# Products of constants in three dense attentions: in the first sequence's preparation, beside the first maxima and beside the last masked steps

## The chip, the cores and the metric

The kernel runs on one core of a Trainium2 chip. A core has TensorE (PE) for matrix products, with a separate path for loading weights (PEld), VectorE (DVE), ScalarE (ACT), GpSimd (POOL) and SyncE (SP), which mostly issues DMAs. Products are written to PSUM, eight banks of 2 KB for each of the 128 partitions; everything else stands in SBUF. The metric is the device time of one execution in microseconds (us). The profile also tells the clock that TensorE was granted, as a share of its full speed.

## What is computed

Four sequences of 512 tokens with 128 features, fp32, go through four layers, each a "ffn" block with a factor one half, an "attn" block and the same "ffn" block again:

```python
x = x + 0.5 * _L1_ffn_ref(_layernorm(x, axis=-1), ...)
x = x + _L1_attn_ref(_layernorm(x, axis=-1), ...)
x = x + 0.5 * _L1_ffn_ref(_layernorm(x, axis=-1), ...)
...
x = x + _L3_attn_ref(_layernorm(x, axis=-1), ...)
```

Two kinds of block hold a dense attention with 16 heads of 8 features. `_L1_ffn_ref` (used twice) is a causal attention with rotary positions, a layer norm, a mixture of eight experts of which each token uses two, and another layer norm:

```python
q_in = _apply_rope(xh, sin, cos).reshape(B, S, E)
q = (q_in @ Wq.T + bq).reshape(B, S, H, D)      # k from q_in too, v from x
scores = jnp.einsum('bqhd,bkhd->bhqk', q, k) * scale
scores = jnp.where(causal[None, None], scores, -inf)
attn = jax.nn.softmax(scores, axis=-1)
ctx = jnp.einsum('bhqk,bkhd->bqhd', attn, v).reshape(B, S, E)
x1 = _layer_norm(x + ctx @ out_proj_w.T + out_proj_b, ln1_w, ln1_b)
```

`_L3_attn_ref` is an attention over all 512 keys, without a mask, with rotary positions on q and k. The other blocks (local and block attentions, linear attention, experts, pattern layers) aren't touched here.

## The kernel before

One function, `dense_attention` (L720 to L872), holds the attention. It is called three times: by `l1_ffn` (L874) for layer 1's first and second ffn (called l1f and l1g below, `masked=True`), and by `l3_attn` (`masked=False`, called l3a). The program is a list of instructions for each engine, in the order in which the Python code issues them, apart from instructions that a scheduler may move on DVE; the products, the transposes and ScalarE's operations marked `by_order` keep the order of the code. Engines wait for each other with semaphores.

The 16 heads are worked four at a time, as 16 units (sequence b, group j). `qT` and `km` hold queries and keys transposed, 32 partitions for each of four heads, so that one 32-row product gives a head's scores. A unit has four steps, one for each tile of 128 keys; a step has two halves of two heads each. The steps of all units make one sequence of 64, and a loop from n = -LEAD (LEAD is 5) to 68 issues, for each n and half:

- `scores(n)`: `pk_at` <- qx, km: scores with keys on the partitions, 512 queries or, when masked, only those from the key tile on (512, 384, 256, 128). One buffer of two banks, "k".
- `maxima(n + 5)`: `pq_at` <- km, qT: scores of one tile of 128 queries in the order 0, 3, 2, 1; DVE takes each row's maximum into `nm` (L757 with the mask in one custom operation, L752 as a plain reduction of two heads without). Two buffers of two banks, "q".
- `weights(n)`: ACT takes the exponential of `pk_at` into `PT` (L787); when masked, POOL cuts the diagonal tile (L790).
- `with_values(n - 1)`: `po_at` <- PT, vh, summed over the four steps in one bank, "o".
- what stands due at this n: `queries` (`pm_at`, transposes of the maxima, then `qx` L768, the queries less their maxima), `end` (`pt_at`, division by the sums), `output`, `project`, the preparation of the next sequence, and the pieces of the next block, whose due times a hand-written plan gives (`tick()`).

PSUM is thus full: `MIX = dict(k=1, q=2, o=1, m=1)`, with two banks for each k and q buffer; "m" serves all the small products.

The preparation of a sequence is a list of functions with due steps. For the second to fourth sequence they are spread over the steps of the sequence before. For the first one, all that are due before step -5 are issued at once ahead of the loop (L849 to L852). In l1f and l1g these are six: `norm` and `scale` (layer norm of x into y), `features` (transposes `pt_y`, copy `yT` L241), `rotate` (`pw` <- yT times a permutation; `qin` on DVE L901 and L905), `queries` (`pq` <- qin, `qT` on ACT L911) and `keys` (`pk` <- qin, `kT` on ACT L917, four masked copies `km`). In l1g the first three find that the layer before has already made y and yT of sequence 0 (`ready`), and issue nothing. In l3a the six are `begin_sequence` (norm, `pt_y`, `yT`), first and second half of the rotated keys (`p` <- yT, DVE L1499 and L1505, POOL L1506), `mark` (km), and the two halves of the queries. `values` (`pv`, `vh` L715) is due at -4 and is issued in the loop.

So in steps -5 to -1 only maxima run, and in steps 59 to 63 (`n_steps - LEAD` and on) no maxima are left, only scores, weights and values, with the experts of the third sequence (`pl`, `pt_g`, `pb`, `pe`, and DVE's weighted sums L997) between them in l1f and l1g. `pe` takes its buffers from "q". In l3a other work of the block's end stands there.

`mm_in_order` (L163) issues a product that keeps its place on TensorE. `onesm` is a 128x128 tile of 1/128, `cst` the packed tile of constants. An fp32 product appears in the trace as two matmul records for each 128x512 product.

Of the kernel before, what the change touches and what calls it, by code (L numbers as in the profile page):

```python
# [29 lines left out]
B, S, D, H, HD = 4, 512, 128, 16, 8  # L30
# [73 lines left out]
def tile_macaron(ctx, tc, x_in, const_in, vec_in, w0_in, ws_in, ws3_in, w2f_in, w3_in, out):  # L104
# [17 lines left out]
    def bank(tag, name):  # L122
        n = 2 if tag in "kqd" else 1
        return psum["pool"].tile([P, n * 512], F32, tag=tag, name=name, bufs=psum["bufs"][tag])
# [10 lines left out]
    cst = keep.tile([P, CONST.n], F32, name="cst")  # L135
# [8 lines left out]
    onesm = keep.tile([P, P], F32, name="onesm")  # L144
# [15 lines left out]
    def transpose(dst, src):  # L160
        return nc.tensor.transpose(dst, src, ident[: src.shape[0], : src.shape[0]])  # L161

    def mm_in_order(dst, lhsT, rhs, start=True, stop=True):  # L163
        tc.keep_in_program_order(nc.tensor.matmul(dst, lhsT=lhsT, rhs=rhs, start=start, stop=stop))  # L164

    def transpose_in_order(dst, src):
        tc.keep_in_program_order(transpose(dst, src))

    def bcast(ap, n):

        return ap[:, :, None].to_broadcast([ap.shape[0], ap.shape[1], n])
# [47 lines left out]
    def by_order(i):  # L219
        if ordered["act"]:  # L220
            tc.keep_in_program_order(i)
# [37 lines left out]
    def tick(busy=False):  # L259
        clock[0] += 1  # L260
        for c in list(chains):
            while c[2] and clock[0] >= c[1] + c[2][0][0] and not (busy and c[2][0][2]):
                busy |= c[2][0][2]
                run(c)
# [415 lines left out]
    LEAD = 5  # L680
# [39 lines left out]
    def dense_attention(sb, prepare, finish, wo, masked, tiles=None):  # L720
# [6 lines left out]
        n_steps = TB * len(units)  # L727
# [3 lines left out]
        def seq(b):  # L731
            if b not in seqs:
                seqs[b] = {"vh": vhs[b % 2], "ao": sb.tile([P, TB, D], F32, tag="ao", name="ao", bufs=2)}
            return seqs[b]

        def maxima(step, half):

            (b, j), qt = units[step // TB], order[step % TB]
            qT, km = seqs[b]["q"], seqs[b]["k"]
            nk = (qt + 1) * P if masked else S  # L740
            pq = bank("q", "pq_at")
            for i in range(2):
                g = half * 2 + i
                mm_in_order(
                    pq[:, i * 512 : i * 512 + nk],
                    qT[32 * g : 32 * g + 32, ts(qt, P)], km[32 * g : 32 * g + 32, j, :nk],
                )
            nm = nms[j % 2]
            if not masked:
                a = nm[:, qt, 0:1]  # L750
                to = bass.AP(a.tensor, a.offset + 64 * half + HD * (j ^ 1), [list(a.ap[0]), [32, 2]])
                nc.vector.tensor_reduce(to, pq.rearrange("p (i n) -> p i n", i=2), AX.X, ALU.max)  # L752
                return
            for i in range(2):
                at = 64 * half + 32 * i + HD * (j ^ 1)
                s = sb.tile([P, S], F32, tag="s", name="s")
                nc.vector.tensor_tensor_reduce(  # L757
                    s[:, :nk], pq[:, i * 512 : i * 512 + nk], causal[:, S - nk :], 1.0, -BIG, ALU.add, ALU.max,
                    nm[:, qt, at : at + 1],
                )  # L760

        def queries(u):
            b, j = units[u]
            pm = bank("m", "pm_at")
            for qt in range(TB):
                transpose_in_order(pm[:, ts(qt, P)], nms[j % 2][:, qt, :])
            qx = sb.tile([P, S], F32, tag="qx", name="qx", bufs=2)
            nc.vector.tensor_add(qx, pm, seqs[b]["q"])  # L768
            qxs[u] = qx

        def scores(step, half):

            u, kt = step // TB, step % TB
            b, j = units[u]
            q0 = kt * P if masked else 0
            pk = bank("k", "pk_at").rearrange("p (i n) -> p i n", i=2)
            for i in range(2):
                g = half * 2 + i
                mm_in_order(
                    pk[:, i, q0:], seqs[b]["k"][32 * g : 32 * g + 32, j, ts(kt, P)], qxs[u][32 * g : 32 * g + 32, q0:]  # L780
                )
            return pk

        def weights(step, half, pk):
            q0 = step % TB * P if masked else 0
            PT = sb.tile([P, 2, S], F32, tag="PT", name="PT", bufs=4)
            by_order(nc.scalar.activation(PT[:, :, q0:], pk[:, :, q0:], AF.Exp, scale=SC8))  # L787
            if masked:
                d = PT[:, :, q0 : q0 + P]
                nc.gpsimd.affine_select(  # L790
                    d, d, pattern=[[0, 2], [1, P]], base=0, channel_multiplier=-1, compare_op=ALU.is_ge, fill=0.0
                )
            PTs[step, half] = PT

        def with_values(step, half):
            u, kt = step // TB, step % TB
            b, j = units[u]
            q0 = kt * P if masked else 0
            if kt == 0 and half == 0:
                pos[u] = bank("o", "po_at")  # L800
            PT = PTs.pop((step, half))
            for i in range(2):
                g = half * 2 + i
                at = (4 * g + j) * VW
                mm_in_order(
                    pos[u][32 * g : 32 * g + 32, q0:], seqs[b]["vh"][:, kt, at : at + 32], PT[:, i, q0:],
                    kt == 0, kt == TB - 1,
                )

        def end(u):  # L810

            b, j = units[u]
            ao, oT = seqs[b]["ao"], oTs.pop(u)
            pt = bank("m", "pt_at")
            for qt in range(TB):
                transpose_in_order(pt[:, ts(qt, P)], oT[:, ts(qt, P)])
            o3 = pt.rearrange("p (n c) -> p n c", c=32)
            rec = sb.tile([P, 16], F32, tag="rec", name="rec", bufs=2)
            nc.vector.reciprocal(rec, o3[:, :, HD])
            nc.vector.tensor_mul(  # L820
                ao.rearrange("p t (g c) -> p (t g) c", c=32)[:, :, HD * j : HD * j + HD], o3[:, :, 0:HD], bcast(rec, HD)
            )

        def output(b):
            pt = bank("m", "pt_ao")
            for t in range(TB):
                transpose_in_order(pt[:, ts(t, P)], seqs[b]["ao"][:, t, :])
            aoT = sb.tile([P, S], F32, tag="oT", name="aoT")
            by_order(nc.scalar.copy(aoT, pt))
            seqs[b]["aoT"] = aoT  # L830

        def project(b):
            po = bank("m", "po_ao")
            for t in range(TB):
                mm_in_order(po[:, ts(t, D)], seqs[b]["aoT"][:, ts(t, P)], wo)
            finish(b, po.rearrange("p (t d) -> p t d", d=D))
            del seqs[b]

        oTs = {}
        for u, (b, j) in enumerate(units):  # L840
            n = TB * u
            later.setdefault((n - 1, 0), []).append(lambda u=u: queries(u))
            later.setdefault((n + 5, 1), []).append(lambda u=u: end(u))
            if j == 3:
                later.setdefault((n + 6, 1), []).append(lambda b=b: output(b))
                later.setdefault((n + 7, 1), []).append(lambda b=b: project(b))
            if j == 0:
                for at, f in prepare(b, seq(b)["vh"], seq(b)):
                    if b or at >= -LEAD:  # L849
                        later.setdefault((n + math.floor(at), int(at % 1 * 2)), []).append(f)  # L850
                    else:
                        f()  # L852

        for n in range(-LEAD, n_steps + 5):
            for half in range(2):
                pk = scores(n, half) if 0 <= n < n_steps else None
                if n + LEAD < n_steps:
                    maxima(n + LEAD, 1 - half)
                if pk is not None:
                    weights(n, half, pk)  # L860
                if 1 <= n <= n_steps:
                    with_values(n - 1, half)
                    if half and n % TB == 0:
                        u = n // TB - 1
                        oTs[u] = sb.tile([P, S], F32, tag="oT", name="oT")
                        by_order(nc.scalar.copy(oTs[u], pos.pop(u)))
                fs = later.pop((n, half), ())
                tick(bool(fs))
                for f in fs:
                    f()  # L870
# [1122 lines left out]
```

## Time and profile before

| what | us |
|---|---|
| median of 4 runs | 2941.87 |
| lowest, highest | 2938.86, 2943.68 |
| the profiled execution | 2939.49 |
| its span | 2937.8 |
| mean granted clock of TensorE | 0.862 |
| busy: PE, PEld | 2277.1 (78%), 1181.2 (40%) |
| busy: DVE, ACT, POOL | 1810.8 (62%), 1245.1 (42%), 911.2 (31%) |

The profile is of one execution; the span runs from its first to its last instruction, and all times of rows are counted from the span's start. In a row of the timeline stand the start, the duration of the group, engine, line, operation, the tile written and the tiles read, their sizes (a product is rows*columns of the weights, then partitions x elements of the result), how many records the group has, and in brackets how long the engine had been idle before it and what ended that. The line of most products is that of the helper (L164, transposes L161), so products are told apart by the tile that they write. A row of windows has the window, its length, the busy time and count of PE, PEld, DVE, ACT and POOL, the granted clock, the DMA share and GB/s.

Where the three attentions lie in the trace: l1f's preparation from 422 us (its first product, `pt_y`), its loop from 436 to 764; l1g's from 911 and 919 to 1261; l3a's from 2125 and 2140 to about 2500.

The chain of work that ended last is 51% PE, 23% DVE, 10% ACT, 8% POOL and 6% issue; its largest parts are `pk_at` (10% of the span), `po_at` (6%) and the exponentials (4%). The largest groups of instructions:

```profile
L787 ACT ACTIVATE PT<-pk_at 128x1024 f32<-128x1024 f32 (+3 forms) x384 | 310.8, 809 | 561.0 <-PE pq_at L164 475.2
L164 PE MATMUL pk_at<-qx,km 32*128 32x512 f32 (+3 forms) x1536 | 373.9, 564 | 61.4 <-ACT PT L787 56.4
L164 PE MATMUL po_at<-PT,vh 128*32 128x512 f32 (+3 forms) x1536 | 338.3, 523 | 3.5 <-POOL PT L790 3.3
L757 DVE CUSTOM_DVE_ANT_0 s<-pq_at,cst 128x384 f32<-128x384 f32 (+3 forms) x512 | 248.6, 486 | 100.0 <-PE pq_at L164 89.1
```

### The profile page before, as it was taken

Reading aid. Unit: us, or ns where it says so; the run is one execution under the profiler, and the core shown is the slowest. Engines: PE = TensorE matmul, PEld = TensorE weight load, DVE = VectorE, ACT = ScalarE, POOL = GpSimd, SP = SyncE. Lnnn points to the kernel's source line nnn. Section 1 sums busy time; section 2 is a strip of 40 time slices with the busy share of each in tenths; the row PEclk is TensorE's granted clock in tenths of the full one; section 3 lists DMA queues with packets and bytes.
Section 4 is the critical chain, followed back from the end, with each engine's and each line's share of the span. In section 5 each row is a group of like instructions: output and inputs, shape, how many; then the busy total and the mean of one; then the engine's idle time right before and its main releaser. Section 6 shows DMA issues by size and latency. Waiting matters only on the chain.

```text
span 2937.8 us, 46900 instructions
## 1 busy us (share of the span) xinstructions
PE 2277.1 (78%) x17558; PEld 1181.2 (40%) x17558; DVE 1810.8 (62%) x4776; ACT 1245.1 (42%) x2682; POOL 911.2 (31%) x1700
## 2 busy tenths in 40 slices
PE   4277538889678898958576678988689999689987
PEld 2145213333333333338456645555322222355553
DVE  4656476676566666554564477777455564677773
ACT  3054303433332433313232266766224444477773
POOL 1022012332122222212321387775100000677661
PEclk8588759999787999768776789999779999899998
DMA  3042010000000000007104510000000000100000
GB/s 133 0 152 81 0 58 1 1 1 1 1 1 1 1 1 4 4 8 266 60 9 168 165 30 22 21 21 14 1 1 1 1 1 1 24 23 20 22 21 11
DMA packets 33771, 99.12 MB, mean 34 GB/s; under 512 B 6184, under 2 KB 12072, under 8 KB 33032
## 3 DMA queue, kind: packets, MB, share of 16 engines
q1 hardware_dynamic: 30616, 88.03, 9.1%
q0 software_dynamic: 2496, 5.12, 0.8%
q8 instruction: 138, 2.26, 0.3%
q10 hardware_dynamic: 432, 2.98, 0.3%
q14 instruction: 89, 0.73, 0.1%
HBM read 66.88 MB, written 14.55 MB: 28 GB/s over the span
## 4 chain that ended last, share of the span: by engine, by line
PE 51%; DVE 23%; ACT 10%; POOL 8%; issue 6%; DMA 1%; POOLq 0%; DVEq 0%; ACTq 0%; SPq 0%
PE pk_at L164 10%; PE po_at L164 6%; ACT PT L787 4%; PE pa L164 3%; PE pag L164 3%; PE po L164 3%; PE pe L164 3%; PE p_qk L164 2%; DVE t L1599 2%; PE pq_at L164 2%; DVE t L1596 2%; PE pg L164 2%; PE pv L164 2%; POOL t L1603 2%; PE pt L161 2%
## 5 line engine op out<-in xcount | busy, mean ns | idle before, releaser
L787 ACT ACTIVATE PT<-pk_at 128x1024 f32<-128x1024 f32 (+3 forms) x384 | 310.8, 809 | 561.0 <-PE pq_at L164 475.2
L164 PE MATMUL pk_at<-qx,km 32*128 32x512 f32 (+3 forms) x1536 | 373.9, 564 | 61.4 <-ACT PT L787 56.4
L164 PE MATMUL po_at<-PT,vh 128*32 128x512 f32 (+3 forms) x1536 | 338.3, 523 | 3.5 <-POOL PT L790 3.3
L757 DVE CUSTOM_DVE_ANT_0 s<-pq_at,cst 128x384 f32<-128x384 f32 (+3 forms) x512 | 248.6, 486 | 100.0 <-PE pq_at L164 89.1
L1548 ACT ACTIVATE s<-s,nm,rn 128x128 f32<-128x128 f32 x512 | 245.5, 483 | 2.4 <-DVE nm L1654 2.2
L790 POOL TENSOR_SCALAR_AFFINE_SELECT PT<-PT 128x256 f32<-128x256 f32 x256 | 107.0, 419 | 431.6 <-ACT PT L787 431.5
L164 PE MATMUL pq_at<-km,qT 32*128 32x384 f32 (+3 forms) x1024 | 226.7, 532 | 12.7 <-DVE nm L757 6.2
L164 PEld LDWEIGHTS pk_at<-qx,km 32*128 32x128 f32 x1536 | 121.8, 193 | 270.3 <-ACT PT L787 205.5
L752 DVE TENSOR_REDUCE nm<-pq_at 128x2 f32<-128x1024 f32 x128 | 156.2, 1225 | 104.3 <-PE pq_at L164 103.8
L1603 POOL TENSOR_TENSOR t<-t,t 128x1024 f32<-128x1024 f32 x64 | 151.3, 2364 | 135.8 <-DVE t L1599 135.4
L161 PE MATMUL pt_y<-ident,y 128*128 128x128 f32 x224 | 55.1, 378 | 156.9 <-DVE y L214 85.4
L164 PE MATMUL pq_at<-km,t 32*128 32x512 f32 x512 | 149.4, 689 | 7.0 <-DVE nm L752 4.9
L164 PE MATMUL p_qk<-w,hT 128*128 128x512 f32 x256 | 141.8, 681 | 11.0 <-DVE t L1599 9.1
L164 PEld LDWEIGHTS po_at<-PT,vh 128*32 128x32 f32 x1536 | 56.2, 110 | 225.4 <-issue 149.1
L161 PE MATMUL pt<-ident,s 128*128 128x128 f32 x640 | 92.8, 292 | 67.4 <-POOL s L1666 35.5
L241 ACT COPY yT<-pt_y 128x512 f32<-128x512 f32 x56 | 32.7, 584 | 258.1 <-PE pt_y L161 211.3
L1666 POOL TENSOR_TENSOR s<-s,sm 128x1024 f32<-128x1024 f32 x64 | 121.4, 1896 | 47.5 <-DVE sm L1665 39.4
L1596 DVE TENSOR_TENSOR t<-p_qk,w 128x1024 f32<-128x1024 f32 x64 | 78.3, 1224 | 70.2 <-ACT sq L1548 69.8
L1548 ACT ACTIVATE sq<-p_qk 128x1024 f32<-128x1024 f32 x64 | 65.5, 1024 | 127.4 <-PE p_qk L164 70.6
L161 PEld LDWEIGHTS pt<-ident,s 128*128 128x128 f32 x640 | 78.3, 150 | 99.6 <-POOL s L1666 52.5
L161 PEld LDWEIGHTS pt_y<-ident,y 128*128 128x128 f32 x224 | 34.9, 173 | 188.5 <-issue 113.1
L1290 DVE SCALAR_TENSOR_TENSOR hT<-pa,w,sg 128x128 f32<-128x128 f32 x184 | 51.8, 345 | 84.8 <-ACT sg L1289 63.9
(424 smaller groups left out, 5196.0 us busy)
## 6 DMA issues: line engine op xcount, KB each, us to landing
w<-in_w2f_dram SPq DMA_DIRECT2D x46, 836.0 KB, 6.3
vb<-v SPq DMA_DIRECT2D x112, 128.0 KB, 2.2
skew<-qe SPq DMA_DIRECT2D x16, 512.0 KB, 3.0
rel<-skew SPq DMA_DIRECT2D x64, 128.0 KB, 3.3
w<-in_w_dram SPq DMA_DIRECT2D x1, 4147.0 KB, 12.3
w<-in_w_dram SPq DMA_DIRECT2D x1, 3200.0 KB
od<-o SPq DMA_DIRECT2D x46, 64.0 KB, 4.7
yd<-y SPq DMA_DIRECT2D x8, 256.0 KB, 2.3
```

Source lines behind the costliest of these rows:

```text
L161: return nc.tensor.transpose(dst, src, ident[: src.shape[0], : src.shape[0]])
L164: tc.keep_in_program_order(nc.tensor.matmul(dst, lhsT=lhsT, rhs=rhs, start=start, stop=stop))
L752: nc.vector.tensor_reduce(to, pq.rearrange("p (i n) -> p i n", i=2), AX.X, ALU.max)
L757: nc.vector.tensor_tensor_reduce(s[:, :nk], pq[:, i * 512 : i * 512 + nk], causal[:, S - nk :], 1.0, -BIG, ALU.add, ALU.max, nm[:, qt, at ...
L787: by_order(nc.scalar.activation(PT[:, :, q0:], pk[:, :, q0:], AF.Exp, scale=SC8))
L790: nc.gpsimd.affine_select(d, d, pattern=[[0, 2], [1, P]], base=0, channel_multiplier=-1, compare_op=ALU.is_ge, fill=0.0)
L1290: nc.vector.scalar_tensor_tensor(hT[s][:, c, :], pa[:, ts(c, P)], b1[:, c : c + 1], sg, ALU.add, ALU.mult)
L1548: tc.keep_in_program_order(nc.scalar.activation(*args, **kw))
L1596: nc.vector.tensor_mul(by_head(t1), by_head(p3), over(tab[:, 0]))
L1599: nc.vector.tensor_mul(by_head(t2[:, :, a]), by_head(p3[:, :, z]), over(tab[:, 1, :, a]))
L1603: nc.gpsimd.tensor_add(t1, t1, t2)
L1666: nc.gpsimd.tensor_mul(s, s, bcast(sm, P))
```

## The change

A helper issues a product of two constants into a fresh PSUM tile that nothing reads, `n` columns wide. `dense_attention` calls it in three places: with 512 columns (S) in bank "o" after each of the six functions of the first sequence's preparation, whether or not the function issued anything; with 256 columns in "o" in both halves of the five steps that have maxima alone; and, in the masked attentions only, with 256 columns in "q" in both halves of the last five steps. In the loop it comes after the maxima and ahead of the weights and of `with_values`. That is 6 + 10 + 10 products in each of l1f and l1g and 6 + 10 in l3a, 68 in all. What the kernel computes stays the same.

```diff
+    def idle_product(tag, n):
+
+        mm_in_order(bank(tag, "idle")[:, :n], onesm, cst[:, :n])
+
...
                         later.setdefault((n + math.floor(at), int(at % 1 * 2)), []).append(f)
                     else:
                         f()
+                        idle_product("o", S)
 
         for n in range(-LEAD, n_steps + 5):
             for half in range(2):
                 pk = scores(n, half) if 0 <= n < n_steps else None
                 if n + LEAD < n_steps:
                     maxima(n + LEAD, 1 - half)
+                if n < 0:
+                    idle_product("o", S // 2)
+                elif masked and n_steps - LEAD <= n < n_steps:
+                    idle_product("q", S // 2)
                 if pk is not None:
                     weights(n, half, pk)
```

## The prediction

> **What bounds the kernel now.** I read the page's forty slices first, then the stretches around the three attentions window by window, then TensorE's timeline inside them.
>
> ```profile
> PE   4277538889678898958576678988689999689987
> PEclk8588759999787999768776789999779999899998
> ```
>
> A slice is 73.4 us. Slices 5 and 28 (about 367 and 2057 us on) hold l1f's preparation and the work ahead of the last attention; the granted clock is 0.5 and 0.7 there, and the whole run's mean is 0.862. So the kernel is bound by chains of products at changing speed, and a stage's start and end are where it is slow. Windows over the tail of the first masked attention (start, length, busy time and instructions of each engine, clock):
>
> ```profile
> 731.37:734.78 3.41, 3.41 (x24) 1.48 (x24) 2.50 (x11) 0.88 (x3) 0.81 (x2) 1.00 0.00 0
> 734.78:738.20 3.42, 2.00 (x14) 0.59 (x12) 2.10 (x11) 1.84 (x2) 0.42 (x1) 1.00 0.00 0
> 738.20:741.61 3.41, 3.15 (x8) 0.69 (x8) 0.00 (x0) 1.49 (x3) 0.81 (x2) 0.50 0.02 5
> 741.61:755.26 13.65, 13.65 (x51) 5.14 (x49) 1.24 (x3) 2.96 (x5) 1.63 (x4) 0.50 0.00 0
> 755.26:758.68 3.42, 3.42 (x6) 1.14 (x4) 0.00 (x0) 0.00 (x0) 0.00 (x1) 0.50 0.00 0
> 758.68:762.10 3.42, 3.42 (x21) 1.28 (x20) 2.37 (x7) 0.38 (x1) 0.41 (x1) 1.00 0.01 2
> ```
>
> After one window with only 2.00 us of products the clock halves, and stays halved for six windows, four of which have PE busy to the last hundredth. TensorE is then the bound, and DVE waits for it:
>
> ```profile
> 755.23 3.68 PE L164 MATMUL pe<-ws,yT 128*128 128x512 f32 x4
> 758.95 2.28 DVE L997 SCALAR_TENSOR_TENSOR y<-pe,g,y 128x128 f32<-128x128 f32 x6 [6.18 <-PE pe L164]
> ```
>
> The other two cold places are the preparations, l1f's and then l1g's on TensorE's timeline, and l3a's end on ScalarE's:
>
> ```profile
> 424.11 2.08 PE L164 MATMUL pw<-yT,cst 128*128 128x512 f32 x2 [0.73 <-ACT yT L241]
> 429.68 2.08 PE L164 MATMUL pq<-qin,ws 128*128 128x512 f32 x2 [3.50 <-DVE qin L905]
> 432.60 2.08 PE L164 MATMUL pk<-qin,ws 128*128 128x512 f32 x2 [0.84 <-ACT qT L911]
> 435.93 0.81 PE L164 MATMUL pq_at<-km,qT 32*128 32x128 f32 x8 [1.26 <-DVE km L693]
> ```
> ```profile
> 910.96 1.12 PE L164 MATMUL pw<-yT,cst 128*128 128x512 f32 x2 [0.38 <-DVE x L1166]
> 913.95 1.13 PE L164 MATMUL pq<-qin,ws 128*128 128x512 f32 x2 [1.86 <-DVE qin L905]
> 915.94 2.08 PE L164 MATMUL pk<-qin,ws 128*128 128x512 f32 x2 [0.86 <-ACT qT L911]
> ```
> ```profile
> 2162.16 1.28 ACT L787 ACT_TABLE_LOAD   x1 [26.43 <-issue]
> 2163.45 1.02 ACT L787 ACTIVATE PT<-pk_at 128x1024 f32<-128x1024 f32 x1
> ```
>
> The same 128x512 product takes 1.12 us at full and 2.08 us at half clock: the step from the second to the third row of l1g is a clock change.
>
> **The rule I take from the rows.** All clock changes in the trace lie on one grid of 3.413 us. I gave every such window a number: the streaming time of its products (two passes of N columns for fp32: 0.85 us for 512 columns at full clock, 1.71 us at half), weighted by the rows they use of 128 (two 32-row products side by side count a half), as a share of the window. Over 860 windows: from half clock the next window is full when the number is at least about 0.75 (242 windows, 65 rises, 2 or 3 misfits); from full clock it stays full when the number is at least about 0.37 (618 windows, 553 stay, at most 6 misfits). 734.78 above has 0.27 and falls; 741.61 to 755.26 has 0.52 to 0.72, PE wholly busy, and stays cold, since 32-row pk_at products count a half; 755.26, wholly 128-row pe, has 0.95 and rises. l1g's tail falls after a window of 0.33, its preparation after 0.25, l3a's after 0.09. One window of 0.78 in l1g's preparation did not rise, so the upper limit isn't sharp.
>
> The Trainium skill ("TensorE: Matmul & The Clock Gate", Part 1, "What's actually happening") gives a free-running window of about 3.4 us and says that a busy one releases the throttle. The grid agrees; busy alone does not, by the 13.65 us of 13.65 at 0.50. Read to the letter, the page speaks against this change: products that are busy anyway would have no more to release, and only their cost would be left, the slower rival's sum below.
>
> **The change, part by part.** It removes nothing. It adds 68 products of 128 rows by constants: 26 in each masked attention, 16 in l3a; 18 of them with 512 columns (2.08 us cold, 1.12 warm, by the rows above) and 50 with 256 (half the streaming: 0.85 cold, 0.43 warm, beside other products). No DMA is moved, and ACT, POOL and SP keep their order. Waits: each product waits for the one before it in its bank, on PE itself; the first of each attention waits for the bank's last reader (l1f DVE's x at 416.8; l1g x from pz_1a at 910.9; l3a yT at 2127.0); in the tail the bank "q" was freed by maxima long past, and the second pe takes the buffer that an idle product has just left, so that it still does not wait for DVE's sums. DVE's order shifts by small operations: in l1f the two qin operations come ahead of five of 0.16 us, one 1.17 us product of vectors goes behind km, and qx in the tail behind 0.4 us.
>
> *A, l1f's preparation.* Two 512-column products run in the 7.95 us in which PE idles before pt_y (422.22): covered. The third delays pw by 1.0, the fourth lies in the 3.50 us before pq. Full-row work from 422 to 428 gives a window of about 0.9 and full clock from 424.8 or 428.2. So pq starts 0.85 earlier, pk takes 1.12 instead of 2.08 and the first pq_at starts at 433.05 instead of 435.93. The maxima then go at DVE's pace: for unit 0, twice 0.68, 1.48, 1.22 and 0.96 (pairs at 128, 512, 384 and 256 keys: 0.34, 0.74, 0.61 and 0.48 each), plus 0.69 for vh: 9.4; a warm pq_at and its idle product (1.06 + 0.43 = 1.49 at 512 keys) just fit under 1.48. After the first 0.8 us, the 0.55 that the moved product costs, and 0.69 for qx with its transposes, pk_at starts near 445.4, before 451.92: the first exponential near 447 against 454.05. **-7** (bounds -3, if the rise comes two windows late, to -8).
>
> *B, l1f's tail.* The two products at steps of 128 columns push the last unit's start from 733.84 to 734.7; the idle 0.84 us of PE in the next two half-steps (2.31 each) covers 0.43. The window that had 0.27 gets 0.43 / 3.41 = 0.13 or more for each product, some 0.46 with one and a half: it holds. From 738.46 to pe's start at 755.23 PE is saturated for 16.8 us cold; warm that is 0.53 of it (pk_at 1.06 against 2.0 from start to start), 8.9, plus five idle products of 0.43 = 2.15. pe starts at 739.3 + 11.05 = 750.4 and takes 1.99 instead of 3.68: ends at 752.3 against 758.9. Less waiting at PT and pb trims or adds a little: **-7** (bounds -5 and -9.4, the latter with all idle products hidden).
>
> *C, l1g's preparation.* Norm, scaling and transposes of sequence 0 were done in the layer before, so three idle products stand in a row behind x and directly delay pw: 1.15 + 1.15 + 0.85 = 3.15. pq is 2.8 later, pk 1.8 (warm now), the first pq_at 921.05 against 919.27: +1.8. The clock holds from there; the maxima take DVE's 9.4 instead of PE's pace, so that the first exponential is at 934.6 instead of 937.64 (-3.0), and the steps to 946.4 run in 2.3 us instead of 3.2 and 2.8 (937.64, 940.84, 943.62, 946.83): another 2.8. **-5.8** (-3 to -7).
>
> *D, l1g's tail.* As B, with the clock held from 1229.72: 1232.1 to 1252.1 is 20 us cold, 10.6 warm, plus six products of 0.43, and pe 1.9 instead of 3.8; with the 0.9 lost at the start, pe ends at 1247.9 against 1255.9. **-8** (-6 to -10.5).
>
> *E, l3a.* The first product delays p by 1.7 cold; the others fill the 0.84 to 0.96 us gaps between the four p at 2127 to 2138 and a little more, until the clock rises near 2130.8 (2129.6 to 2133): first pq_at 2140.1, before 2140.18. Then a half-step is 1.28 (pq_at 0.85 + 0.43; the reduction's 1.23 fits under it) against 1.7 cold: first exponential 2157.3 against 2163.45, and the cold steps up to 2171.8 save 2.3 more (2.31 instead of 3.20 each). Against it: the 1.28 us table load leaves PE idle for 2.3 us, and with 4 chances in 10 a window falls under 0.37 there and costs 2.5 back. **-7** (-2 to -9).
>
> Cover: where the clock is not raised, none of the products is free; that is the slower rival. **Sum:** -7 -7 -5.8 -8 -7 = -34.8. The profiled execution took 2939.49 us (span 2937.8 and 1.7 around it), 2.4 under the median 2941.87; 2939.5 - 34.8 = 2904.7, and 2.4 more gives **2907**.
>
> **Rivals.**
> *Slower: idle products don't count as activity* (constants, or a busy measure that the cold stretches already fill). The point is the window after 734.78: if it falls although a product lies in it, their cost is bare. Preparations: l1f 1.0 + 1.2 + 0.8 (products of 2.08 in gaps of 0.84 and 1.26 after pq and pk), l1g 3.15 + 1.2 + 0.8, l3a 1.7 + 3 x 1.2: 13.5. Maxima: ten times 0.85 into some 3.9 us of gaps of PE between 435.9 and 451.9: 4.6, l1g 5, l3a 2.5: 12. Tails: ten times 0.85 less some 1 us of gaps: 7.5 each, 15. Sum +40: **2982**. For it: the wholly busy yet cold windows, whose reason I have only inferred; against it: 755.26, whose one long 128-row product did raise the clock.
> *Half of it: either the tails or the preparations give nothing*, because 256 columns land in the wrong window (0.33 and 0.27 are near 0.37, but a product also delays work out of its window) or a late rise leaves the preparation paying for its products: -15 to -20, **2924**.
> *No change:* the rise pays exactly for the products; at the prices above (35 gained, 40 lost) that is when about half of the windows rise: **2942**.
>
> **How the numbers follow.** All five places 0.66, half 0.18, no change 0.05, slower 0.11. The likeliest case alone goes from 2897 to 2922 (its bounds sum to -19 and -44; all at one end is unlikely). The range that leaves out 2 in 10 has to take in the half case: 2895 to 2931. A measurement of this kernel tells about 0.2% (5.9 us) from no change: the four runs before span 4.8 us. Faster 0.84, same 0.05, slower 0.11.
>
> **What would show it.** Right: clock 1.00 through 738 to 759 and 1230 to 1257 (moved by the earlier gains), pk of l1g at 1.1 us, the first exponential of l1f some 7 us earlier, DVE's wait before L997 under 1 us. Wrong: the clock falling in those windows with the idle products inside; pq_at half-steps in the preparation longer than before; pw of l1g 3 us later with the exponential not earlier; new waits of pq_at on bank "q" in the tail.

## The result

The changed kernel took 2936.91 us by the median of 44 runs (2914.07 to 2949.18), the kernel before 2940.35 by 69 (2924.87 to 2950.54): a ratio of 0.9986 with a 95% interval of 0.9976 to 0.9995. The medians differ by 3.4 us. The prediction was 2907. A second set of runs, below, gave 0.9975 (0.9959 to 0.9990). The profiled execution took 2930.48 us with a span of 2928.8; the mean granted clock is 0.883 where it was 0.862. So the clock was raised as forecast, and most of the time that it should have bought is missing.

The granted clock of the changed kernel in forty slices of its span, from the page:

```profile
PEclk8578769998889999969777799999799999899998
```

In the clock row the sixth slice (l1f's preparation) has 6 for 5, and the ten slices from the seventh on, with l1f and l1g in them, sum to 87 tenths for 85. l1f's tail, windows on the grid of this execution (columns as before):

```profile
732.75:736.17 3.42, 3.42 (x20) 1.37 (x20) 2.84 (x13) 0.87 (x2) 0.41 (x1) 1.00 0.00 0
736.17:739.58 3.41, 2.99 (x19) 1.15 (x18) 0.38 (x2) 2.04 (x3) 0.82 (x2) 1.00 0.00 0
739.58:753.23 13.65, 13.65 (x70) 5.43 (x66) 1.24 (x3) 3.78 (x6) 2.04 (x5) 1.00 0.00 0
753.23:756.65 3.42, 3.42 (x19) 1.43 (x18) 2.45 (x7) 0.39 (x1) 0.41 (x1) 1.00 0.03 7
```

The stretch that was at 0.50 is at 1.00. TensorE is still busy to the last hundredth: a part of what the clock gave is filled by the products themselves. The same place on the timeline, and l1f's and l1g's preparations:

```profile
751.32 1.99 PE L164 MATMUL pe<-ws,yT 128*128 128x512 f32 x4
753.34 2.67 DVE L1006 SCALAR_TENSOR_TENSOR y<-pe,g,y 128x128 f32<-128x128 f32 x7 [4.27 <-PE pe L164]
```
```profile
425.34 1.12 PE L164 MATMUL pw<-yT,cst 128*128 128x512 f32 x2
...
429.88 1.12 PE L164 MATMUL pq<-qin,ws 128*128 128x512 f32 x2 [2.56 <-DVE qin L914]
...
431.84 1.12 PE L164 MATMUL pk<-qin,ws 128*128 128x512 f32 x2
...
440.63 0.92 PE L164 MATMUL pq_at<-km,qT 32*128 32x384 f32 x4
441.47 0.70 PE L164 MATMUL idle<-cst,onesm 128*128 128x256 f32 x2
442.10 0.91 PE L164 MATMUL pq_at<-km,qT 32*128 32x384 f32 x4
```
```profile
905.51 3.49 PE L164 MATMUL idle<-cst,onesm 128*128 128x512 f32 x6 [0.38 <-DVE x L1175]
908.84 1.02 PE L164 MATMUL pw<-yT,cst 128*128 128x512 f32 x2
...
911.44 1.13 PE L164 MATMUL pq<-qin,ws 128*128 128x512 f32 x2 [0.72 <-DVE qin L914]
...
913.43 1.13 PE L164 MATMUL pk<-qin,ws 128*128 128x512 f32 x2
```

All 128x512 products take 1.0 to 1.1 us. From the start of a 256-column product to the next product it is 0.63 us (441.47 to 442.10), not the 0.43 of its streaming. l1g's three products in a row delay pw by 3.33 us (905.51 to 908.84). The two rows of DVE say that it starts its sums at 753.34 and had waited 4.27 us, where it was 758.95 and 6.18; the prediction's sign of being right was a wait under 1 us.

The table below compares every profile with the first one of the kernel before, place by place. Each number is how much longer (+) or shorter a stretch is, taken from the start times of the same ScalarE instruction at its ends (at 423, 460, 725, 776, 895, 965, 1217, 1263, 2113, 2189 and 2490 us of the first profile); "rest" is the start, the blocks from 1263 to 2113 and all from 2490 to the end.

| profile | A l1f prep. | l1f loop | B l1f tail | linear att. | C l1g prep. | l1g loop | D l1g tail | sum | E l3a prep. | l3a loop | rest | span |
|---|---|---|---|---|---|---|---|---|---|---|---|---|
| changed, 1st | -5.5 | +2.6 | -2.9 | -0.9 | -3.5 | 0.0 | -6.8 | -16.9 | +1.0 | +2.8 | +4.0 | -9.0 |
| 2nd (e1_again) | -5.5 | +2.5 | -2.9 | -0.9 | -3.5 | -0.1 | -6.7 | -17.0 | +14.5 | 0.0 | +2.6 | +0.1 |
| 3rd (e12_again) | -5.5 | +1.5 | -5.3 | +0.5 | -0.5 | -4.2 | -6.8 | -20.3 | -2.8 | +2.8 | +3.6 | -16.7 |
| 4th (e13_again) | -5.5 | +1.3 | -5.2 | +0.5 | -0.5 | -4.2 | -6.8 | -20.5 | +14.0 | 0.0 | +5.1 | -1.3 |
| before, 2nd (b1) | 0.0 | +0.7 | -7.1 | +1.0 | +1.4 | -5.7 | -2.4 | -12.2 | +0.9 | 0.0 | -1.8 | -13.1 |
| before, 3rd (b2) | 0.0 | +0.7 | -7.1 | +1.0 | +1.4 | -4.3 | -1.9 | -10.2 | 0.0 | 0.0 | +0.8 | -9.4 |
| before, 4th (b3) | 0.0 | 0.0 | 0.0 | 0.0 | -0.5 | -4.8 | -1.6 | -6.9 | +0.1 | 0.0 | +0.4 | -6.4 |
| e2_masked_only | -5.5 | +2.5 | -2.9 | -0.9 | -3.5 | 0.0 | -6.8 | -16.9 | +0.9 | 0.0 | +9.5 | -6.4 |
| e4_tails_only | 0.0 | 0.0 | -4.5 | -0.8 | +1.1 | -2.6 | -6.8 | -13.6 | +0.2 | 0.0 | +7.2 | -6.1 |
| e5_no_tails | -5.5 | +2.6 | -7.0 | +1.1 | -0.5 | -4.1 | -0.1 | -13.5 | +14.3 | 0.0 | +7.3 | +8.1 |
| e10_l3a_only | 0.0 | 0.0 | 0.0 | 0.0 | 0.0 | 0.0 | 0.0 | 0.0 | +1.0 | +2.8 | +4.9 | +8.8 |
| e6_bridge | -5.5 | +1.3 | -5.3 | +0.5 | -0.5 | -4.1 | -6.8 | -20.4 | -2.6 | +2.8 | +9.0 | -11.2 |
| e7_32rows | +5.7 | +3.8 | -4.1 | +2.7 | +12.5 | 0.0 | -5.7 | +14.9 | +3.2 | 0.0 | +6.3 | +24.4 |
| e8_masked_lean | -4.2 | -2.2 | -4.1 | -1.8 | -6.4 | -1.6 | -6.8 | -27.3 | +1.1 | 0.0 | +5.3 | -20.9 |
| e14_lean_again | -6.6 | 0.0 | -4.6 | -1.0 | -6.4 | -1.6 | -6.8 | -27.0 | +0.2 | 0.0 | -7.0 | -33.9 |
| e9_lean_bridge | -6.6 | +0.8 | -3.0 | -2.9 | -6.4 | -3.3 | -7.7 | -29.2 | -5.9 | +2.8 | +10.8 | -21.4 |
| e11_lean_tail128 | -4.3 | -0.5 | -5.4 | -2.0 | -8.0 | -3.8 | -3.2 | -27.2 | +0.2 | 0.0 | +12.4 | -14.7 |

"Sum" is from A to D. The profiles of changed kernels have the labels of the experiments below. "The number" below is that of the prediction: the streaming time of a 3.413 us window's products, weighted by the rows of 128 that they use, as a share of the window. How products at a window's edge are counted moves it by up to 0.02.

### The profile page after: what moved, and what is told of

The parts are those of the page before. It is cut to its first block, busy times and chain, and to the rows that moved or that the text cites. A ratio compares the mean times of both kernels' runs of the same rounds, so it can differ in the third digit from the quotient of the medians.

```text
span 2928.8 us, 47171 instructions
## 1 busy us (share of the span) xinstructions
PE 2288.0 (78%) x17694; PEld 1189.3 (41%) x17694; DVE 1811.2 (62%) x4776; ACT 1246.2 (43%) x2682; POOL 913.9 (31%) x1700
## 4 chain that ended last, share of the span: by engine, by line
PE 51%; DVE 22%; ACT 11%; POOL 8%; issue 6%; DMA 2%; POOLq 0%; DVEq 0%; ACTq 0%; SPq 0%
PE pk_at L164 10%; PE po_at L164 6%; ACT PT L791 4%; PE pag L164 3%; PE pa L164 3%; PE po L164 3%; PE pe L164 3%; PE p_qk L164 2%; DVE t L1608 2%; DVE t L1605 2%; PE pg L164 2%; PE pq_at L164 2%; POOL t L1612 2%; PE pt L161 2%; PE pv L164 2%
## 5 line engine op out<-in xcount | busy, mean ns | idle before, releaser
L164 PE MATMUL pk_at<-qx,km 32*128 32x512 f32 (+3 forms) x1536 | 361.3, 547 | 59.7 <-ACT PT L791 54.9
L164 PE MATMUL po_at<-PT,vh 128*32 128x512 f32 (+3 forms) x1536 | 330.3, 512 | 3.5 <-POOL PT L794 3.3
L164 PE MATMUL pq_at<-km,qT 32*128 32x128 f32 (+3 forms) x1024 | 215.8, 498 | 7.7 <-DVE y L1006 4.0
```

## The experiments

**The changed kernel again**, three times: e1_again with twelve timed runs, e12_again and e13_again with one profiled execution each. No edit.

> The changed kernel once more, for a second profile. In its first profile the five places had gained 5.5 (l1f's preparation), 4.8 (l1f's tail), 3.5 (l1g's preparation), 6.8 (l1g's tail) and lost 1.0 (l3a), 19.6 us in all, but the span was only 9 us shorter; l1f's loop lost 3.6, l3a's loop 2.8 and the last block 3.7. Theory (phase): the places gain the same again within 1.5 us each, while the stretches that the change doesn't touch lose other amounts at other steps, because the clock falls there in windows that depend on where the free-running grid lies. Rival (fixed cost): the loops lose the same 3.6 and 2.8 at the same steps, so that the products leave something behind that the loop pays for.

> The changed kernel a third time, for l3a. Theory: either about 1 us or about 14 us lost in l3a, by the window over the pause (at least 0.37 or below), nothing between; l1f's preparation again -5.5, l1g's -3.5, l1g's tail -6.8. Rival: other losses in l3a, without a tie to that window.

> The changed kernel a fourth time, as the third: about 1 or about 14 us lost in l3a, by the window over the pause or by a window that rises through pv.

e1_again: 2933.57 us median of 12, ratio 0.9975 (0.9959 to 0.9990). The expectation's 4.8 in l1f's tail and 3.6 in its loop were taken at other instructions than the table's -2.9, +2.6 and -0.9, which add up to the same. The places repeat to 0.1 us in A (four times -5.5) and in D. They do not in B (-2.9 twice, then -5.3 and -5.2) and in C (-3.5 twice, then -0.5 twice, with l1g's loop at 0.0 and then -4.2), where -3.5 was expected again. l1f's loop is longer by 2.6, 2.5, 1.5 and 1.3, against 0.0 to 0.7 in the kernel before, so part of the rival holds: A's gain is partly lost again in the loop behind it. l3a costs +1.0, +14.5, -2.8 and +14.0, nothing between. The clock over the pause between the last p and the first pq_at of l3a tells them apart. The second profile, windows:

```profile
2118.03:2121.45 3.42, 3.29 (x9) 1.14 (x7) 2.02 (x4) 1.52 (x2) 0.14 (x1) 1.00 0.00 0
2121.45:2124.86 3.41, 2.09 (x8) 0.60 (x6) 0.84 (x2) 0.00 (x0) 1.26 (x1) 1.00 0.00 0
2124.86:2155.58 30.72, 30.72 (x67) 11.89 (x66) 12.66 (x12) 0.00 (x0) 0.00 (x0) 0.50 0.00 1
```

The third profile:

```profile
2117.78:2121.19 3.41, 2.09 (x7) 0.49 (x5) 0.75 (x1) 0.00 (x0) 1.26 (x1) 1.00 0.00 0
2121.19:2138.26 17.07, 17.07 (x70) 7.21 (x68) 12.71 (x12) 0.00 (x0) 0.00 (x0) 1.00 0.00 1
```

TensorE is busy 2.09 us of the window both times. The number is 0.35 in the second profile, and the clock falls; it is 0.41 in the third, and it holds. In the first (0.38) and the fourth (0.37) it fell too, so the limit here lies at about 0.4, a little above the prediction's 0.37. Once fallen, the steps of maxima by themselves don't raise it. On the second profile's timeline:

```profile
2124.92 2.08 PE L164 MATMUL pq_at<-km,t 32*128 32x512 f32 x4
2126.93 1.22 PE L164 MATMUL idle<-cst,onesm 128*128 128x256 f32 x2
2128.08 2.08 PE L164 MATMUL pq_at<-km,t 32*128 32x512 f32 x4
```

A half-step is 3.16 us (2124.92 to 2128.08), TensorE is busy all the time, and the window's number is 0.53 to 0.63, under 0.75. It went on for 30.7 us. The same half-step at full clock in the third profile, and then four of them in the kernel before, cold and without a product (a row with x8 holds two):

```profile
2120.19 1.13 PE L164 MATMUL pq_at<-km,t 32*128 32x512 f32 x4 [1.32 <-POOL t L1515]
2121.25 0.70 PE L164 MATMUL idle<-cst,onesm 128*128 128x256 f32 x2
2121.88 1.13 PE L164 MATMUL pq_at<-km,t 32*128 32x512 f32 x4
```
```profile
2147.59 2.09 PE L164 MATMUL pq_at<-km,t 32*128 32x512 f32 x8
2151.00 3.21 PE L164 MATMUL pq_at<-km,t 32*128 32x512 f32 x8 [1.31 <-DVE nm L752]
```

With a product at full clock it is 1.69 us (1.06 for pq_at and 0.63 for the product); without one at half clock it is 1.70 (3.41 for two). In the first profile a window with all of pv reached 0.76 at 2132 us and the clock rose; in the fourth pv's best window had 0.70 and it did not. From the first transposes to the first exponential l3a took 38.3 us before; here 40.4, 51.2, 35.6 and 51.3.

**The masked attentions only** (e2_masked_only):

```diff
                         f()
-                        idle_product("o", S)
+                        if masked:
+                            idle_product("o", S)
...
-                if n < 0:
+                if masked and n < 0:
```

> The products in l3a left out. Theory (the 256-column product takes 0.63 us of TensorE and not 0.43, so a warm half-step of l3a is 1.06 + 0.63 = 1.69 and a cold one without it 1.70): l3a is no slower than with them, by 0 to 3 us faster, from first transposes to first exponential 38.3 us as before against 40.4 with them; the whole 0 to 3 us under the changed kernel. Rival (l3a's gain was there and was hidden by one unlucky clock fall at 2125 us): the whole 3 to 7 us slower than the changed kernel.

2928.10 us median, six runs from 2926.39 to 2933.06, ratio 0.9955 (0.9940 to 0.9970): some 5 us under the changed kernel in the same set of runs (2933.57), and much closer together (the changed kernel went from 2925.34 to 2945.56). The theory had 0 to 3. That it is a little more fits l3a's loss of 14 us in two of the four profiles of the changed kernel. Here l3a took 38.7 us.

**l3a only** (e10_l3a_only; the conditions the other way round, no tails):

> Only l3a's sixteen products. Theory (they hold the clock only if the window over the pause before the first pq_at reaches 0.37, and can't raise it again): l3a costs 1 us more than before where it holds or rises early, 14 us more where it falls; everything ahead of 2108 us is as before, and the whole is 5 to 14 us slower than before by the median. Rival (l3a's loss came from the earlier products, by another phase): l3a costs within 2 us of before, and so does the whole.

2942.09 us median of 12, ratio 1.0019 (1.0002 to 1.0035): slower, by 4 us in the medians and by 0.6 to 10 in the ratio's interval, where 5 to 14 were expected. The stretches from A to D stayed as they were. The profiled execution was like the changed kernel's first: number 0.38, clock fallen, raised by pv at 0.76; l3a +1.0 and its loop +2.8. So l3a's products are a loss by themselves, without the others.

**Tails only, and no tails** (e4_tails_only, e5_no_tails: the products of the other places left out):

> Only the products of the last five masked steps, 20 in all. Theory: l1f's tail gains 5 and l1g's 7 in the profile, the rest as before; the whole 8 to 12 us under the kernel before if the stretches between give nothing back. Rival (what is gained is given back in the work behind, whose clock falls instead): both tails gain, the blocks behind them lose it within 100 us, and the whole is within 4 us of before.

> The products of the preparations and of the steps of maxima, all three attentions, no tails. Theory: l1f's preparation gains 5.5, l1g's 3.5, l3a loses 1 to 3; the tails are cold as before; the whole 5 to 8 us under before. Rival (a loop that begins without a clock rise lies at another phase to the grid and loses several us in its steps): the loops of l1f and l1g lose 5 us or more against before, and the whole is not faster than before.

Tails only: 2930.78 us, ratio 0.9967 (0.9951 to 0.9982), -4.5 and -6.8 in the tails; by the ratio 9.7 us under before, as expected, and nothing of it lost within 100 us behind l1f's tail (-0.8). No tails: 2934.31 us, 0.9981 (0.9967 to 0.9996), 5.6 us by the ratio. A is as elsewhere; l3a lost 14.3 in this profile where 1 to 3 were expected. And l1f's tail, expected cold as before, is 7.0 shorter without any product in it, more than with them (-2.9 to -5.3): where it now met the grid, the clock fell in another window, and a later one rose early. The kernel before, below, shows the same tail at 0 or at -7.1 by itself, so one profile doesn't tell whether the products in l1f's tail bring anything on the mean. In l1g's tail they do: -0.1 without, -6.8 with, and 0 to -2.4 in the kernel before.

**One more product over l3a's pause** (e6_bridge):

```diff
                         f()
                         idle_product("o", S)
+                        if not masked and at == -9:
+                            idle_product("o", S)
```

> The changed kernel with one more 512-column product behind the last function of l3a's preparation. In three profiles with l3a's products, first transposes to first exponential of l3a cost 40.4 us in one and about 53 us in the other two: there the clock fell in the window over the 1.3 us pause before the first pq_at (number 0.35 to 0.38), and the ten half-steps with a 256-column product then went 3.16 us each at half clock with the number 0.53 to 0.63, too low to rise. Theory (hold but not raise): the extra product lifts that window to 0.55 or more, the clock holds, the ten half-steps go at 1.69, first exponential 37 us after the first transposes; no run has the 14 us, so the whole is 7 to 12 us under the changed kernel and its runs lie closer together. Rival (the clock falls for another reason than the window's number, or a half-step can't hold it either): l3a is cold again, 50 us or more, and the whole is within 2 us of the changed kernel.

2922.74 us, ratio 0.9945 (0.9924 to 0.9966). The windows over the pause and the maxima:

```profile
2120.25:2123.66 3.41, 3.21 (x10) 0.79 (x8) 0.75 (x1) 0.00 (x0) 1.26 (x1) 1.00 0.00 0
2123.66:2140.73 17.07, 17.07 (x72) 7.15 (x72) 12.87 (x12) 0.00 (x0) 0.00 (x0) 1.00 0.00 1
```

The number is 0.63 where it was 0.35 to 0.41, the clock holds, the half-steps go at 1.69, and the first exponential comes 35.6 us after the first transposes. One product of 0.85 us that fills a pause saves up to 17 us in this stretch (-2.6 for +14.5), some 14 with the loop behind it. The six runs lie 13 us apart (2915.40 to 2928.55), where twelve of the changed kernel lay 20 apart; the ratio lies 9 to 12 us under the changed kernel's two (0.9975 and 0.9986), where 7 to 12 were expected. The theory of the window fits all of this, and the rival's cold l3a and unchanged time did not come.

**The same products with 32 rows** (e7_32rows):

```diff
-        mm_in_order(bank(tag, "idle")[:, :n], onesm, cst[:, :n])
+        mm_in_order(bank(tag, "idle")[:, :n], onesm[:32], cst[:32, :n])
```

> The same 68 products with 32 of the 128 rows (contraction over 32 partitions), so that their time stays and their rows are a quarter. Theory (the number weights rows): the clock falls in l1g's tail as before and stays at half there, and the preparations stay cold too, since 0.15 a window becomes 0.04; both tails are slower than before by 3 to 6 us each, the whole 10 to 40 us slower than before. Rival (busy time counts): nothing changes against the changed kernel, clock 1.00 in l1g's tail.

2963.88 us in one run (before: 2940.16 by the median of 11), +24 by the profile. l1f's and l1g's preparations are 5.7 and 12.5 us longer than before, although at the same clock a product takes the same time on TensorE (2.07 us for 512 columns at half clock):

```profile
919.72:923.13 3.41, 2.95 (x16) 1.18 (x8) 2.42 (x11) 0.27 (x1) 1.26 (x1) 1.00 0.00 0
923.13:943.61 20.48, 20.42 (x40) 7.22 (x40) 6.63 (x24) 4.66 (x6) 1.27 (x1) 0.50 0.00 1
```

TensorE is busy 2.95 of 3.41 us at full clock, and the clock falls all the same (number 0.26); it then stays at half while TensorE is busy 20.42 of 20.48 us. So busy time does not decide, and rows count. The expectation of the tails was wrong: l1g's clock did fall, but rose again within 7 us, and both tails were 4 to 6 us shorter than in the first profile of before.

**Lean** (e8_masked_lean, and again as e14_lean_again): masked attentions only, no product behind a function that issues nothing, 128 columns beside the maxima.

```diff
                         f()
-                        idle_product("o", S)
+                        if masked and not (at <= -16 and seqs[b].get("ready")):
+                            idle_product("o", S)
...
-                if n < 0:
-                    idle_product("o", S // 2)
+                if masked and n < 0:
+                    idle_product("o", S // 4)
```

> Masked attentions only, without the products after functions that issue nothing (three in l1g), and 128 columns instead of 256 beside the maxima; tails unchanged. Theory (a product takes 0.2 us of TensorE besides its streaming, so 0.42 instead of 0.63): a maxima half-step at 512 keys goes from 1.69 to 1.48, l1f's preparation gains 1 to 2 us more than 5.5, l1g's 3.0 + 1 to 2 more than 3.5, and the clock still holds; the whole 2 to 6 us under the kernel with the masked attentions alone. Rival (the clock needs the wider ones): it falls in the maxima steps, where half-steps take 2.1 and more, and the preparations are no faster than before.

> The lean masked kernel once more, for its size: again 0.989 to 0.994 of the kernel before, its runs within 8 us of each other, since nothing in it hangs on l3a's window.

2916.28 us (six runs, 2910.96 to 2918.57), ratio 0.9923 (0.9904 to 0.9943), and again 2914.53, 0.9935 (0.9912 to 0.9957). By the medians this is 23 to 24 us under the kernel before in the same sets of runs, and by some 20 under the changed kernel. The second time the runs lay 24 us apart (2905.63 to 2930.02), not within 8. The gain over e2 was 9 to 12 us (by the ratios and by the medians, in different sets of runs) where 2 to 6 were expected. Of the 3.33 us in l1g 2.9 came back (C -6.4 for -3.5). The products are cheaper:

```profile
438.74 0.91 PE L164 MATMUL pq_at<-km,qT 32*128 32x384 f32 x4
439.58 0.49 PE L164 MATMUL idle<-cst,onesm 128*128 128x128 f32 x2
440.00 0.92 PE L164 MATMUL pq_at<-km,qT 32*128 32x384 f32 x4
```

0.42 us from start to start with 0.21 of streaming, as 0.63 with 0.43 above: the rest, 0.2, comes with every group of products whatever its width. Narrow is near the limit: in e8's l1f the clock fell once beside the maxima, after a window of 0.37 (A -4.2), and the second time it did not (-6.6). Of the rest of the gain the most lies in the loops (l1f's -2.2 and 0.0 for +2.5, l1g's -1.6 for 0.0), whose clock falls in other windows than in e2; no run shows why they came out shorter.

**Lean with l3a bridged, lean with narrow tails** (e9_lean_bridge, e11_lean_tail128):

> As the lean one, and in l3a the six products, one more behind the last function, and 128 columns beside the maxima. Theory: l3a's clock holds over the pause, half-steps go at 1.48 instead of 1.70 cold, first exponential 4 to 6 us earlier than before; the whole 3 to 6 us under the lean masked one. Rival (128 columns don't hold l3a): half-steps of 2.6 us, l3a 8 us slower than before.

> The lean masked kernel with 128 columns in the tails too. Theory (a product adds 0.06 instead of 0.13 to its window, 0.42 us instead of 0.63 to TensorE): where the tail's lowest window stays at 0.37 or more (it was 0.44 with 256 columns), each tail gains 1 us more than the lean kernel; where it falls below, the tail goes cold and loses 4 to 7 us. By 0.44 less some 0.06 to 0.12 it is near the limit: the whole within 4 us of the lean kernel either way. Rival (tail products aren't needed at this phase): the tails lose nothing at all.

e9: 2917.59 us, 0.9932 (0.9910 to 0.9955). l3a's start gains 5.9 where 4 to 6 were expected, its loop loses 2.8, and the whole, expected 3 to 6 us lower, is not told from e8. e11: 2925.06, 0.9952 (0.9934 to 0.9969). l1g's tail falls after a window of 0.37, and its gain is 3.2 instead of 6.8; l1f's tail held with about the same (0.38). From A to D the sum is e8's (-27.2), and what makes this kernel 5 to 9 us slower than the lean one lies, in its profile, in the rest (+12.4), which holds no product of the tails.

**The kernel before again**, three more profiled executions, for what was still open:

> The kernel before, for a second profile of it. Theory (the first profile had a short last block by chance): the stretches that no experiment touches (start, between 1263 and 2113 us, and from 2490 us to the end) are 3 to 9 us longer here than in the first, as they are in all twelve later profiles, and other stretches are shorter. Rival (what is gained ahead is given back in the blocks behind): these stretches are within 2 us of the first profile.

> The kernel before a third time; as the second. The places that the change touches should show how much they vary by themselves: l1f's and l1g's, ahead of 1263 us, within 1 us of the first profile, l3a by up to 3 us.

> The kernel before a fourth time, as the second and third: the untouched stretches 3 to 9 us longer than in the first profile, the others alike.

They took 2926.44, 2930.05 and 2933.11 us. The theory was wrong: the end from 2700 us was indeed 3.1 to 3.3 longer each time, but the blocks between 1263 and 2113 us were 3.4 to 5.5 shorter, so the rest as a whole is within 2 us of the first profile, as the rival said. That leaves the rival's reason (gains given back in the blocks behind) possible: the rest is +2.6 to +12.4 in every profile with products but one (e14, -7.0). No run tests it. What no expectation had: l1f's and l1g's places are 7 to 12 us shorter than in the first profile with nothing changed. l1f's tail in the second profile of before:

```profile
735.63:739.04 3.41, 2.57 (x16) 0.89 (x16) 2.96 (x15) 1.41 (x2) 0.83 (x3) 1.00 0.00 0
739.04:745.87 6.83, 6.23 (x22) 1.31 (x18) 0.53 (x3) 2.31 (x3) 0.81 (x2) 0.50 0.01 2
745.87:756.11 10.24, 10.24 (x62) 4.30 (x63) 2.61 (x7) 3.35 (x6) 2.03 (x5) 1.00 0.00 1
```

The clock fell here too, but rose after 6.8 us instead of 20.5: a window happened to hold enough 128-row work (0.81) early. Two of four profiles of before had this tail 7.1 us shorter, without any product.

## Why the prediction was wrong

**The clock rule was right.** With the two limits of the prediction (0.75 to rise, 0.37 to stay) the first profile of the changed kernel has one to three misfits in some 200 cold windows and four in 651 warm ones; the most in any profile are nine and eight, so the limits are sharp to a few hundredths only. Weighting by rows times columns of the weights, which no run tries, fits worse in the same trace: 14 and 16 misfits with the best limits, and 6 and 14 for streaming time without a weight. 32 rows instead of 128 took the effect away in the preparations; one product in the right window held the clock in l3a. That a busy window releases the clock, as the Trainium skill has it ("TensorE: Matmul & The Clock Gate", Part 1, "What's actually happening"), does not fit the busy time measured here: 20.42 us of 20.48 at half clock. In the prediction's own reading of the rows, five of the six cold windows of l1f's tail are busy to the last hundredth, not four.

**Step E failed.** It read: "Then a half-step is 1.28 (pq_at 0.85 + 0.43; the reduction's 1.23 fits under it) against 1.7 cold", for -7 (-2 to -9). A warm half-step with its product is 1.69 (1.06 and 0.63 from start to start), as much as a cold one without (1.70): the products buy l3a nothing beside the maxima. And the step took the clock as held once it had risen. It asked for the number of a window only at the table load, where it put 4 chances in 10 and 2.5 us; the pause before the first pq_at decides (1.3 us here, 2.18 in the trace of before), at 0.35 to 0.41, over 14 to 17 us. The four profiles give, with l3a's loop, +3.8, +14.5, 0.0 and +14.0, a mean of +8.1 in place of -7: 15 of the 31 us that are missing. That l3a's products cost time is shown by leaving all others out (e10, slower than before), by leaving them out (e2, 5 us faster) and by the bridged pause (e6).

**The base was one draw.** Steps B, C and D took the cold stretches of the one profile as what the kernel pays each time. In the four profiles of before the stretch from A to D is 0, 12.2, 10.2 and 6.9 us shorter than in that one, 7.3 on the mean: 0 in A, 3.6 in B, 3.1 in C with l1g's loop, 1.5 in D. The changed kernel's means are -5.5, -4.1, -4.1 and -6.8. Against the mean of before, A and D keep their gains, and B and C bring 1 us or less each. How much of this holds for all executions is open: the three later ones took 2926 to 2933 us, less than the median of 2940, which the first (2939.49) is near. The four timed runs that the prediction went by lay 4.8 us apart; 69 lie 25.7 apart.

**The product was mis-sized.** "0.43 warm, beside other products" is 0.63: the 0.2 us that each group costs, which the rows of pq_at (1.06 for 0.85) had shown, was left out. In A and C it turned DVE's pace into TensorE's: from 430 to 447 us of the changed kernel TensorE is busy 16.60 of 17.00 us, DVE 13.73. Against the first profile of before, A is -5.5 for -7, B -2.9 to -5.3 for -7, C with l1g's loop -3.5 to -4.7 for -5.8, D -6.8 for -8. In A and D the mechanism was right and the gain 21% and 15% short; in B and C much of it can be the draw. A's own terms also add up to 444.5 us for pk_at's start, and not to its 445.4. The three products in l1g cost 3.33 us, forecast at 3.15.

**Stretches were taken as independent.** l1f's loop is 1.3 to 2.6 us longer in every profile with A's products as in the changed kernel (-2.2 to +0.8 with the lean ones) and 0.0 to 0.7 in those of before, though nothing in it changed. In the first profile of the changed kernel it keeps step with before to 0.6 us for its first 170 us; from there the clock falls in other windows, after 174 and 212 us of the loop instead of 165 and 179. That the grid's phase does this is read off the windows; no run set the phase by itself, so it is not shown.

Together, against the first profile: -18.7 from A to D for the forecast -27.8, +8.1 in l3a and its loop for -7, and +3.8 in the rest for nothing. That makes the four spans 6.7 us shorter on the mean, where the medians of 44 and 69 runs say 3.4. Against the mean of the four profiles of before the same places give -11.4, +7.8 and +4.0, or +0.5 us. So l3a's 15 us stand by either base. Of the other 16, the first profile puts 9 into A to D (B 2.9, l1f's loop 2.0, C with l1g's loop 1.7, A 1.5, D 1.2) and 4 into the rest, which has no explanation; how much of this is the draw, four profiles of each kernel don't tell.

Of the rivals, "no change" (2942) was nearest, given 1 chance in 20, but not for its reason: the clock was full through both tails and from the start of both masked preparations on, and the largest part of what cancels their gain is l3a. "Half of it" (2924) had the right kind of loss, a preparation that pays for its products, but by a late rise; here the clock rose in time and fell again. The slower rival is out: the products did count, and only the 32-row ones came near its price (+24 of 40).

## What to carry to other kernels

A product that nothing reads can hold the clock where it stands in a pause; beside 32-row work that already filled TensorE at half clock, 256 columns did not raise it. So fill the pause ahead of such a stretch, with few and narrow products, and leave out those behind functions that issue nothing. Before pricing a cold stretch as a fixed cost, take several profiles of the unchanged kernel: here the same stretch was cold for 6.8 us or for 20.5. A group of products is priced from start to start, since the part that streaming does not explain (0.2 us) is the same for a narrow one.

## What the runs showed of the hardware

The clock's rise and its fall have different limits (about 0.75 and 0.37 of a 3.41 us window, in weighted streaming time), which makes two stable states of the same code: l3a's ten half-steps with a product each ran at 1.69 us at full clock and at 3.16 at half, TensorE busy throughout in both. They stayed in the state in which they began, unless other products raised the window (pv, to 0.76, in the first profile).
